# Five re-orderings in a four-layer network kernel: stacks at every step, v's products ahead of scores, sums for two groups, two copies on one engine, the mix ahead of transposes

## The chip, the cores and the metric

The kernel runs on one core of a Trainium2 chip, in single precision. The metric is the device time of one execution in microseconds. The core has five engines with queues of their own: TensorE (PE, matrix products and transposes, which write to eight PSUM banks), VectorE (DVE), ScalarE (ACT), GpSimd (POOL) and SyncE (SP), which here issues nearly all DMAs. Each engine takes its instructions in the order in which they were put into its queue.

## The reference

An input x of shape (2, 1024, 1024) passes through four layers. Each layer is an attention-like block and a feed-forward block, and each block ends in `x = layernorm(x + block(x))`. Cut to what the change touches:

```python
# layer 0, attention: 8 heads of 16, keys from all 1024 rows
qk = (x @ Wqk_w.T + Wqk_b).reshape(b, n, H, E, 2)          # q and k
v = (x @ Wv_w.T + Wv_b).reshape(b, n, H, E)
attn = softmax(einsum('bhqd,bhkd->bhqk', q, k)) / sqrt(128)
out = einsum('bhsl,bhlv->bhsv', attn, v) @ Wo_w.T + Wo_b
# layer 0, feed-forward: columns of x permuted, 16 blocks of up, gelu, down
# layer 1, attention: a convolution of width 3 over the rows (1024 -> 768), then attention in
# blocks of 128 rows with 16 heads of 64, output and projection
# layer 1, feed-forward: softmax router over 8 experts scales the input and output channels of
# x @ sign(weight).T
# layer 2: a selective state-space scan, then an int4 weight product
# layer 3, attention: one head of width 256 over 1024 rows
attn = softmax(einsum('bqd,bkd->bqk', q, k) / 16)
out = einsum('bqk,bkd->bqd', attn, v) @ Wo + bo
# layer 3, feed-forward: x @ base_W.T + b and low-rank experts weighted by the router's ranks
```

## The kernel before

The two batches run one after the other through all layers. A batch's x lies in SBUF as eight row tiles of 128 x 1024 (`x`), and a transposed copy as `xT` (eight column groups `k` of 128 by 1024 rows). `to_xT(tt)` makes the transposed copy of one row tile: eight PE transposes into two PSUM banks, and two copies out by `evac`, which gives them to DVE and ACT in turn. Inside a stage the order of the calls in the program is the order of the instructions on every engine; the stages are written out by hand. `ps()` takes one of the eight PSUM banks.

**Layer 0, attention (`l0`).** `qkv(s, th, scalar)` makes k, q or v (s = 1, 0, 2) for half th of the rows: eight k, two matmuls each, and gives way after every second k. The q and k parts are then spread over 32-row strips by eight small DMAs. `side` is the list of such pieces that are still to be made when the scores begin, one list entry for each step of a piece. `maxima(th)` makes the scores and their row maxima in 16 steps: in each, four matmuls of a step to come into four banks and four DVE reductions of the present one. The loop over n runs these steps and takes one piece of `side` after each (two in the first two steps). `attend(th, extra)` then makes scores again, exponentials and outputs in 16 steps, and runs the functions in `extra[n]` at step n: for th = 0 the steps of `maxima(1)`, for th = 1 (the second pass) the output projection, layernorm and `to_xT` of the first four row tiles. At the end of the second pass four stores `xd<-xT` put these tiles into DRAM, one at each of its steps 6 to 9, and at step 9 eight indirect DMAs on POOL (`gather(0)`) read them back with permuted columns (`t<-xd`). `blocks(th, ...)` is the feed-forward part; its first products need the first of these. Each of its blocks ends in a scatter to `yd` from POOL.

**Stacks.** In batch 0 alone, `stacks()` prepares layer 1's convolution weights: in 24 rounds it loads three pieces of 128 x 256 by SP, forms four sums with eight POOL operations, and stores them to the DRAM tensor `cvd` by SP. It is a generator of 26 steps: one loads, 24 store the round before, load the next and make the present one, and the last stores. It works in two sets of buffers. It is driven by `next(made)` at chosen steps of `maxima(0)`, of the first pass and of the second pass.

**Layer 1, attention (`l1_attn`).** The convolution is done in fast form. `sums(th, steps, k0, k1)` makes the input combinations on DVE, called `one`, `two`, `three` and so on; tile 1 of `one` is a + 2 and tile 2 becomes 2 - a. `product(co, j)` multiplies combination j with the weights of output group co over eight k (PE, line 740). At the start of the stage the tiles 4 to 7 of x still wait for their layer-0 output: it comes by scatters into `yd`, a reload into `vh`, and transposes in `add_y(tt, ys)`. Weights come through a ring of eight buffers. At the end `join(1)` makes the second half's outputs, and `to_xT(3)` and the first router product of `l1_ffn` (line 118, over tiles 0 to 3) follow.

**Layer 3 (`late_rest`).** For each of the eight row tiles: `scores`, `exps` (softmax with the maximum), `turn` (transposes of the weights into `pts`, copies by ACT). `mix(th)` multiplies `pts` of four tiles with v (32 matmuls in two banks, copies by `evac`), `join(wo, tt)` makes the output projection and adds it to x, `stats(tt)` makes mean and reciprocal root (DVE, then Ln and Exp on ACT, then four small DVE operations, line 186 first), `ln_scale(tt)` applies them on DVE, and `turn_x(tt)` is `to_xT(tt)` and the adding of a row vector on POOL (line 143). `route(0)` needs tiles 0 to 3 of `xT`.

Of the kernel before, what the change touches and what calls it, by code (L numbers as in the profile page):

```python
# [21 lines left out]
NT = S // P  # L22
# [5 lines left out]
class Net:  # L28
# [98 lines left out]
        if b < B:  # L127
            self.nc.sync.dma_start(self.x[:, tt, :], self.i["x"][b, tt * P : (tt + 1) * P, :])

    def to_xT(self, tt):  # L130
        nc = self.nc
        for g in range(2):
            p = self.ps()
            for j in range(4):
                k = 4 * g + j
                nc.tensor.transpose(p[:, j * P : (j + 1) * P], self.x[:, tt, k * P : (k + 1) * P], self.ident)  # L136
            self.evac(
                self.xT[:, 4 * g : 4 * g + 4, 1 + tt * P : 1 + (tt + 1) * P],
                p.rearrange("p (k t) -> p k t", k=4),
            )  # L140
# [79 lines left out]
    def l0(self, b):  # L220
        nc, i = self.nc, self.i
# [15 lines left out]
        with self.tc.tile_pool(name=self.nm("l0a"), bufs=1) as lp, self.tc.tile_pool(name=self.nm("l0b"), bufs=2) as tp:  # L237
# [346 lines left out]
            def at(extra, n, f):  # L584
                extra.setdefault(n, []).append(f)

            got = {}
            with self.tc.manual_schedule():
                self.table()
                for s in (1, 0):  # L590
                    for _ in qkv(s, 0, False):
                        pass
                for tt in range(4, NT):
                    self.to_xT(tt)
                for tt in range(4, NT):
                    self.add_row(row, tt)
                side = [
                    f for s, th in ((1, 1), (0, 1), (2, 0), (2, 1)) for f in [qkv(s, th, True)]
                    for _ in range(5 if s == 2 else 4)
                ]  # L600
                m0 = maxima(0)
                for n in range(16):
                    next(m0)
                    if b == 0 and n == 6:
                        made = stacks()
                    if b == 0 and n >= 6 and n % 3:
                        next(made)
                    for f in side[: 2 if n < 2 else 1]:
                        next(f)
                        del side[0]  # L610
                for f in side:
                    next(f)
                m = maxima(1)
                turns = {n: [lambda: next(m)] for n in range(16)}
                turns[0].insert(0, lambda: next(m0))
                if b == 0:
                    for n in range(16):
                        if n % 3:
                            turns[n].append(lambda: next(made))
                done0 = attend(0, turns)  # L620
                e = line(0, project, (0, 1, 3, 4, 5, 6, 7, 8, 9))
                e[0].insert(0, lambda: next(m))
                if b == 0:
                    for n in range(16):
                        if n % 3 < 2 and n < 14:
                            at(e, n, lambda: next(made))
                for n in range(4):
                    at(e, 6 + n, lambda n=n: store(n))
                at(e, 9, lambda: gather(0))
                ahead = {n: [lambda tt=tt: turn_o(tt)] for tt, n in enumerate((0, 1, 3, 4))}  # L630
                done = attend(1, e, ahead, lambda: done0(1))
                e = line(1, project, (0, 0, 1, 1, 2, 3, 3, 4, 4))
                for n, tt in ((3, 4), (3, 5), (4, 6), (4, 7)):
                    at(e, n, lambda tt=tt: store(tt))
                for n in (5, 6):
                    at(e, n, lambda: gather(1, 2))
# [14 lines left out]
    def l1_attn(self, b, yd, op):  # L651
        nc, i = self.nc, self.i
        row = self.row("l1_projb")
        with self.tc.tile_pool(name=self.nm("l1a"), bufs=1) as lp, self.tc.tile_pool(name=self.nm("l1s"), bufs=2) as spool:
# [47 lines left out]

            d = [("d", n) for n in range(6)]

            one = [(2, d[2], -4, d[4]), ("a", d[1], -4, d[3]), (1, "a", 1, 2), (2, "a", -1, 2)]
            two = [(4, d[2], -1, d[4]), ("b", d[1], -1, d[3]), (3, "b", 2, 4)]
            c_, e_ = ("c", d[2], -1, d[0]), ("e", d[3], -1, d[5])
            three, five = [(0, "c", 4, 4), (4, "b", -2, 4)], [(5, "b", -4, "e")]
# [86 lines left out]
            def product(co, j):  # L795
                c[co]["calls"](j)
# [5 lines left out]
            with self.tc.manual_schedule():  # L802
                if b == 0:
                    nc.vector.tensor_scalar(cb6, cb, -6.0, None, ALU.mult)
                    nc.vector.tensor_scalar(bq8, bq, 0.125, None, ALU.mult)
                for co, j in (
                    [(co, j) for j in (1, 2, 3, 0, 4) for co in (0, 1)] + [(2, 1), (2, 2), (2, 3), (0, 5), (1, 5)]
                    + [(2, 4), (2, 0), (2, 5)] + [(co, j) for co in (3, 4, 5) for j in ORDER]
                ):
                    c[co]["load"](j)  # L810
                pump()
                ys = [t for q in range(4) for t in (vh[:, q, :HALF], vh[:, q, HALF:])]
                for k, t in enumerate(ys):
                    nc.sync.dma_start(t, yd[k * P : (k + 1) * P, :])
                for k0, k1 in ((0, 2), (2, 4), (4, KD)):
                    sums(0, one, k0, k1)
                    c[0]["calls"](1, k0, k1)
                product(1, 1)
                product(0, 2)
                product(1, 2)  # L820
                sums(0, two)
                product(0, 3)
                product(1, 3)
                sums(0, [c_] + three)
                self.add_y(4, ys)
                root(4)
                product(0, 0)
                product(1, 0)
                self.add_y(5, ys)
                product(0, 4)  # L830
                c[0]["both"]()
                product(1, 4)
                c[1]["both"]()
                self.to_xT(4)
                sums(0, [e_] + five)
                root(5)
                for j in (1, 2, 3):
                    product(2, j)
                self.add_y(6, ys)
                for co in (0, 1):  # L840
                    product(co, 5)
                    c[co]["last"]()
                self.to_xT(5)
                root(6)
                product(2, 4)
                self.add_y(7, ys)
                product(2, 0)
                c[2]["both"]()
                product(2, 5)
                c[2]["last"]()  # L850
                self.to_xT(6)
                root(7)
                later = {
                    (3, 4): [lambda: self.to_xT(7)], (3, 5): [lambda: sums(1, [c_] + one)], (4, 2): [lambda: sums(1, two)],
                    (4, 4): [lambda: sums(1, [e_])], (5, 2): [lambda: sums(1, three + five)],
                }
                for co in (3, 4, 5):
                    for j in ORDER:
                        product(co, j)
                        if j == 0:  # L860
                            c[co]["both"]()
                        for f in later.get((co, j), []):
                            f()
                    c[co]["last"]()
# [171 lines left out]
            with self.tc.manual_schedule():  # L1036
# [49 lines left out]
                for tt in range(3):  # L1086
                    self.add_row(row, tt)
                join(1, wo)
                self.to_xT(3)
                self.add_row(row, 3)  # L1090
                early.append(row)
        return lambda tt, nh: project(tt, nh, wp), early
# [711 lines left out]
    def turn_x(self, tt, row):  # L1804

        self.to_xT(tt)
        self.add_row(row, tt)
# [243 lines left out]
    def late_rest(self, b, lp, tp, qk, v):  # L2051
        nc, i = self.nc, self.i
        NR = 15
        if True:
# [166 lines left out]
            with self.tc.manual_schedule():  # L2221
# [6 lines left out]
                for n in range(1, NT + 1):  # L2228
                    exps(n - 1)
                    if n >= 7:  # L2230
                        self.ln_scale(n - 7)
                    if n < NT:
                        scores(n)
                    if n == 5:
                        mix(0)
                    if n >= 6:
                        join(wo, n - 6)
                        stats(n - 6)
                    if n == NT:
                        join(wo, 3)  # L2240
                    turn(n - 1)
                    if n >= 7:
                        turn_x(n - 7, row)
                self.ln_scale(2)
                stats(3)
                turn_x(2, row)
                self.ln_scale(3)
                mix(1)
                turn_x(3, row)
                probs = route(0)  # L2250
                join(wo, 4)
# [161 lines left out]
```

## Time and profile before

| | us |
|---|---|
| median of 3 runs | 4809.61 (4804.67 to 4822.28) |
| the profiled execution's own time | 4813.16 |
| its span, from first to last instruction | 4811.4 |
| PE busy | 4440.4 (92%), mean granted clock 0.973 |
| DVE busy | 3331.1 (69%) |
| POOL busy | 2278.4 (47%) |
| ACT busy | 2031.3 (42%) |

The profile is that of one execution. Its timeline gives, for every group of like instructions, the start and the duration in us, the engine, the line of the kernel, the operation, output and inputs, the shape, the count, and in brackets how long the engine had been idle before and which engine's instruction or DMA ended that. "SPq" rows are DMAs that SyncE issues; their duration is that of the issuing. A table by windows gives the busy time of PE, weight loading (PEld), DVE, ACT and POOL in a stretch, the clock that TensorE was granted (1.00 is full), the share of the DMA engines' time, and GB/s.

### The profile page before, as it was taken

The numbers are of one execution on the slowest core, as the hardware profiler recorded it, in microseconds if no ns is written. First come the engines' busy times: TensorE is split into PE (matmuls) and PEld (weight loads), VectorE is DVE, ScalarE is ACT, GpSimd is POOL, SyncE is SP. The second block draws the span as 40 slices with busy tenths as digits, with TensorE's granted clock in tenths as the row PEclk, the third lists the DMA queues.
The fourth block names the chain that finished last, engine by engine and source line by source line (L and its number), as shares of the span: only waits on it lengthen the run. The fifth ranks groups of instructions, "written<-read, shape, count | busy, mean of one in ns | idle before, by whom it ended". The sixth has DMA issues, their size and how long they took to land.

```text
span 4811.4 us, 52825 instructions
## 1 busy us (share of the span) xinstructions
PE 4440.4 (92%) x17736; PEld 2192.6 (46%) x17736; DVE 3331.1 (69%) x4568; ACT 2031.3 (42%) x4131; POOL 2278.4 (47%) x1469
## 2 busy tenths in 40 slices
PE   9899999988898889999999999998888888899999
PEld 4367655333333333564443776553333333335644
DVE  5564276399999997645365643744999999966553
ACT  2432342577675653122025223325776756521310
POOL 5822121288798985030021121304888989841310
PEclk9999999999998999999999999999999999999999
DMA  4565314588888998310121742125888899993100
GB/s 154 158 225 174 108 63 136 146 220 226 237 217 236 252 253 262 127 56 37 53 71 56 244 160 81 64 96 148 223 226 235 210 246 253 246 287 97 54 13 31
DMA packets 315507, 768.08 MB, mean 160 GB/s; under 512 B 40288, under 2 KB 112096, under 8 KB 315236
## 3 DMA queue, kind: packets, MB, share of 16 engines
q1 hardware_dynamic: 307556, 739.52, 53.4%
q0 software_dynamic: 7680, 25.17, 1.6%
q8 instruction: 142, 2.33, 0.2%
q14 instruction: 129, 1.06, 0.1%
HBM read 644.75 MB, written 100.93 MB: 155 GB/s over the span
## 4 chain that ended last, share of the span: by engine, by line
PE 52%; DVE 17%; DMA 10%; issue 5%; POOL 5%; ACT 4%; SPq 1%; POOLq 0%; DVEq 0%; ACTq 0%
PE ps L110 15%; DVE h L1524 9%; PE ps L740 5%; PE ps L2206 5%; PE ps L1896 5%; POOL h L1510 3%; DMA h<-dxd 3%; PE ps L1632 2%; PE ps L1909 2%; PE ps L1850 2%; DVE h L1535 2%; DMA xi<-xcd 2%; PE ps L1546 2%; PE ps L136 1%; PE ps L1517 1%
## 5 line engine op out<-in xcount | busy, mean ns | idle before, releaser
L1510 POOL TENSOR_TENSOR h<-h,br 128x1024 f32<-128x1024 f32 x512 | 1206.2, 2373 | 108.4 <-DMA h<-dxd 68.8
L1519 ACT ACTIVATE ps<-ps,l_Alog 128x512 f32<-128x512 f32 x1024 | 663.1, 662 | 552.8 <-PE ps L1517 550.2
L1517 PE MATMUL ps<-hl,rep 128*128 128x512 f32 x1024 | 733.0, 720 | 171.7 <-DVE h L1524 142.1
L1524 DVE TENSOR_TENSOR_SCAN h<-ps,hst,h 128x512 f32<-128x512 f32 x512 | 628.5, 1263 | 23.0 <-ACT ps L1519 18.4
L1535 DVE TENSOR_TENSOR h<-h,ps 128x1024 f32<-128x1024 f32 x512 | 609.4, 1190 | 2.5 <-ACT hst L1532 2.4
L1524 DVE TENSOR_TENSOR_SCAN h<-ps,h 128x512 f32<-128x512 f32 x512 | 597.1, 1203 | 19.0 <-ACT ps L1519 19.0
L1632 PE MATMUL ps<-xT,w 128*128 128x512 f32 x1024 | 541.2, 614 | 9.4 <-DVE h L1524 8.2
L1517 PEld LDWEIGHTS ps<-hl,rep 128*128 128x128 f32 x1024 | 200.4, 197 | 593.7 <-DVE h L1524 424.8
L143 POOL TENSOR_TENSOR x<-x,row 128x1024 f32<-128x1024 f32 x80 | 190.8, 2406 | 572.5 <-PE ps L136 547.5
L949 POOL TENSOR_TENSOR s<-s,l1r 128x512 f32<-128x512 f32 x64 | 66.3, 1041 | 542.7 <-DVE l1r L948 500.4
L1670 PE MATMUL ps<-w,w 128*128 128x512 f32 x512 | 280.3, 632 | 23.3 <-DMA w<-yd 14.9
L1546 PE MATMUL ps<-h,sel 128*32 128x512 f32 x2048 | 294.8, 628 | 6.7 <-DVE h L1535 6.7
L1455 POOL TENSOR_TENSOR e<-e,one 128x512 f32<-128x512 f32 x64 | 81.6, 1275 | 434.7 <-ACT xp L1327 313.4
L1632 PEld LDWEIGHTS ps<-xT,w 128*128 128x128 f32 x1024 | 188.7, 193 | 200.8 <-issue 163.9
L1577 PE MATMUL ps<-xT,w 128*128 128x512 f32 x512 | 272.3, 631 | 6.2 <-DVE h L1524 6.2
L1335 DVE SCALAR_TENSOR_TENSOR ps<-xp,l_convw,ps 128x512 f32<-128x512 f32 x192 | 144.8, 754 | 183.8 <-ACT ps L1330 179.3
L158 DVE TENSOR_TENSOR x<-x,ps 128x512 f32<-128x512 f32 x192 | 128.6, 681 | 183.8 <-PE ps L2212 136.2
L1896 PE MATMUL ps<-w,w 128*128 128x512 f32 x512 | 228.3, 593 | 0.0
L183 ACT ACTIVATE rs<-mv 128x1 f32<-128x1 f32 (+2 forms) x78 | 15.9, 203 | 502.6 <-DVE mv L177 502.2
L2206 PE MATMUL ps<-w,xT 128*128 128x512 f32 x512 | 225.9, 593 | 0.0
L110 PE MATMUL ps<-xT,w 128*128 128x512 f32 x512 | 225.1, 592 | 0.0
L371 DVE TENSOR_REDUCE mx<-ps 128x1 f32<-128x512 f32 x256 | 158.8, 682 | 46.0 <-PE ps L361 46.0
(320 smaller groups left out, 7788.5 us busy)
## 6 DMA issues: line engine op xcount, KB each, us to landing
h<-dxd SPq DMA_DIRECT2D x512, 512.0 KB, 7.8
w<-l_in SPq DMA_DIRECT2D x128, 512.0 KB, 6.1
w<-cvd SPq DMA_DIRECT2D x96, 512.0 KB, 4.2
w<-l_out SPq DMA_DIRECT2D x96, 512.0 KB, 8.1
w<-l_conv SPq DMA_DIRECT2D x48, 512.0 KB, 4.2
w<-l_fw SPq DMA_DIRECT2D x32, 512.0 KB, 5.4
xcd<-xo SPq DMA_DIRECT2D x64, 256.0 KB, 6.5
xi<-xcd SPq DMA_DIRECT2D x64, 256.0 KB, 8.6
```

The lines of the kernel that those rows point to most:

```text
L110: self.nc.tensor.matmul(out, lhsT, rhs, start=j == 0, stop=j == n - 1)
L1510: nc.gpsimd.tensor_tensor(hs[k], hs[k], norms[of(k)[0]][1].unsqueeze(1).to_broadcast([P, 2, HALF]), ALU.mult)
L1517: nc.tensor.matmul(dA[k, m], rep[:, 4 * m + q, :], hl[u, c][:, jj, :], start=True, stop=True)
L1519: nc.scalar.activation(dA[k, m], dA[k, m], AF.Exp, scale=A[:, g : g + 1])
L1524: nc.vector.tensor_tensor_scan(hs[k][:, m, :], dA.pop((k, m)), hs[k][:, m, :], hst[:, g : g + 1] if u else 0.0, ALU.mult, ALU.add)
L1535: nc.vector.tensor_tensor(hs[k], hs[k], norms[of(k)[0]][3].unsqueeze(1).to_broadcast([P, 2, HALF]), ALU.mult)
L1546: nc.tensor.matmul(py[u, c][32 * j : 32 * j + 32, :], self.sel[:, q, :], hs[k - 1 + j // 2][:, j % 2, :], start=False, stop=q == 3,)
L1577: nc.tensor.matmul(p, w["w"][:, k * P : (k + 1) * P], self.xcols(k, u0, HALF), start=k == 0, stop=k == KD - 1)
L1632: nc.tensor.matmul(p, w["w"][:, k * P : (k + 1) * P], self.xcols(k, u * HALF, HALF), start=k == 0, stop=k == KD - 1)
L1670: nc.tensor.matmul(p, y[:, cc, t * P : (t + 1) * P], wt[:, cc * HALF : (cc + 1) * HALF], start=c2 == 0 and cc == 0, stop=last,)
L1896: nc.tensor.matmul(pa[tt], y[:, cc * HALF + tt * P : cc * HALF + (tt + 1) * P], w[:, cc * HALF : (cc + 1) * HALF], start=c2 == 0 and cc == ...
L2206: nc.tensor.matmul(p, self.xcols(k, tt * P, P), wt[k][:, ns], start=k == 0, stop=False)
```

## The change

Five places are re-ordered; nothing that is computed changes.

1. `stacks()` is advanced at every step from step 6 of `maxima(0)` on and at every step of the first pass, and no more in the second pass. Before it was advanced at two steps of three in all three places. (Batch 0.)
2. The first three steps of v's first half (six of its eight k) are run ahead of `maxima(0)`; the list `side` keeps its length, so that its last entries for this piece do nothing. (Batch 0.)
3. In layer 1, each of the three portions of sums is followed by the products of two output groups, not one, and the fourth sum of `one` (now `less`) is made after the three portions, over all k at once.
4. `to_xT(3)` at the end of layer 1's attention uses DVE for both copies.
5. In layer 3, `mix(1)` is put ahead of the layernorm and transposes of tiles 2 and 3, and at the last step `stats(2)` behind `turn(7)`.

```diff
-    def to_xT(self, tt):
+    def to_xT(self, tt, evac=None):
...
-            self.evac(
+            (evac or self.evac)(
...
+                if b == 0:
+                    for _ in range(3):
+                        next(side[8])
                 m0 = maxima(0)
                 for n in range(16):
                     next(m0)
                     if b == 0 and n == 6:
                         made = stacks()
-                    if b == 0 and n >= 6 and n % 3:
+                    if b == 0 and n >= 6:
                         next(made)
                     for f in side[: 2 if n < 2 else 1]:
-                        next(f)
+                        next(f, None)
                         del side[0]
...
                 if b == 0:
                     for n in range(16):
-                        if n % 3:
-                            turns[n].append(lambda: next(made))
+                        turns[n].append(lambda: next(made))
                 done0 = attend(0, turns)
                 e = line(0, project, (0, 1, 3, 4, 5, 6, 7, 8, 9))
                 e[0].insert(0, lambda: next(m))
-                if b == 0:
-                    for n in range(16):
-                        if n % 3 < 2 and n < 14:
-                            at(e, n, lambda: next(made))
                 for n in range(4):
                     at(e, 6 + n, lambda n=n: store(n))
                 at(e, 9, lambda: gather(0))
...
-            one = [(2, d[2], -4, d[4]), ("a", d[1], -4, d[3]), (1, "a", 1, 2), (2, "a", -1, 2)]
+            one = [(2, d[2], -4, d[4]), ("a", d[1], -4, d[3]), (1, "a", 1, 2)]
+            less = [(2, "a", -1, 2)]
...
                 for k0, k1 in ((0, 2), (2, 4), (4, KD)):
                     sums(0, one, k0, k1)
                     c[0]["calls"](1, k0, k1)
-                product(1, 1)
+                    c[1]["calls"](1, k0, k1)
+                sums(0, less)
                 product(0, 2)
...
-                    (3, 5): [lambda: sums(1, [c_] + one)],
+                    (3, 5): [lambda: sums(1, [c_] + one + less)],
...
-                self.to_xT(3)
+                self.to_xT(3, nc.vector.tensor_copy)
...
                     if n >= 6:
                         join(wo, n - 6)
-                        stats(n - 6)
+                        if n < NT:
+                            stats(n - 6)
                     if n == NT:
                         join(wo, 3)
                     turn(n - 1)
+                    if n == NT:
+                        stats(2)
                     if n >= 7:
                         turn_x(n - 7, row)
+                mix(1)
                 self.ln_scale(2)
                 stats(3)
                 turn_x(2, row)
                 self.ln_scale(3)
-                mix(1)
                 turn_x(3, row)
                 probs = route(0)
```

More of the change, by code (lines that the diff above doesn't have):

```diff
@@ L605, in l0 @@
                         made = stacks()
-                    if b == 0 and n >= 6 and n % 3:
+                    if b == 0 and n >= 6:
                         next(made)
                     for f in side[: 2 if n < 2 else 1]:
-                        next(f)
+                        next(f, None)
                         del side[0]
                 for f in side:
-                    next(f)
+                    next(f, None)
                 m = maxima(1)
@@ L853, in l1_attn @@
                 later = {
-                    (3, 4): [lambda: self.to_xT(7)], (3, 5): [lambda: sums(1, [c_] + one)], (4, 2): [lambda: sums(1, two)],
+                    (3, 4): [lambda: self.to_xT(7)], (3, 5): [lambda: sums(1, [c_] + one + less)], (4, 2): [lambda: sums(1, two)],
                     (4, 4): [lambda: sums(1, [e_])], (5, 2): [lambda: sums(1, three + five)],
```

## The prediction

> **What bounds the kernel now.** I read the page first: one core, TensorE (PE) busy 92% of the span, so a change that only reorders its work can win no more than the idle pieces in front of the moved steps, and half-speed stretches of its clock. The span against which everything below is summed:
>
> ```profile
> span 4811.4 us, 52825 instructions
> ```
>
> Then the timeline of PE, for the five places. A row is start, duration, engine, line, operation, count, and in brackets the idle time before it and what ended that.
>
> ```profile
> 32.74 5.63 PE L361 MATMUL ps<-kT,qT 32*128 32x512 f32 x16 [4.67 <-DMA qT<-st]
> 220.90 3.79 PE L514 MATMUL ps<-t,w 64*128 64x512 f32 x8 [9.66 <-DMA t<-xd,idx]
> 313.02 13.05 PE L740 MATMUL ps<-qh,w 128*128 128x128 f32 x88 [1.92 <-DVE qh L699]
> 653.39 2.05 PE L118 MATMUL ps<-xT,l_gate 128*32 128x512 f32 x16 [0.35 <-DVE xT L103]
> 2232.55 1.97 PE L136 MATMUL ps<-ident,x 128*128 128x128 f32 x8 [5.96 <-DVE x L192]
> ```
>
> These are the first scores (4.67 us), the first blocks (9.66), the sums (1.92, after pieces of 2.23 and 1.08), the router (0.35) and the layernorm chain of the last attention (5.96). The first two are in batch 0 alone; the others recur about 2389 us later. Third, the timelines of GpSimd (POOL) and of the DMA queue (SPq) before the largest wait, and one stretch of the table by windows:
>
> ```profile
> 140.00:160.00 20.00, 18.39 (x155) 7.11 (x153) 12.81 (x26) 8.52 (x17) 18.54 (x25) 1.00 0.45 143
> ```
>
> ```profile
> 210.42 2.14 SPq L280 DMA_DIRECT2D w<-l_conv  x3
> 212.68 0.38 SPq L486 DMA_DIRECT2D xd<-xT  x1
> 214.38 0.72 POOL L291 TENSOR_TENSOR w<-w 128x256 f32<-128x256 f32 x1
> 216.92 1.18 POOL L496 DMA_INDIRECT t<-xd,idx  x1 [1.82 <-DMA xd<-xT]
> 226.86 0.83 POOL L284 TENSOR_TENSOR w<-w 128x256 f32<-128x256 f32 x1
> 239.25 0.73 POOL L291 TENSOR_TENSOR w<-w 128x256 f32<-128x256 f32 x1
> ```
>
> In 20 us POOL (the fifth pair) is busy 18.54; the rest is 0.08 us between operations. The stacks run back to back on it from 71.13: 22 of 24 stand ahead of the gather at 216.92, the last two (226.86 to 239.98) behind it.
>
> **Stacks at every step.** No operation is added. Before, calls stood at 6 + 10 + 10 steps; now at 10 + 16, all 26 before the second attention pass begins. So POOL has 24 stacks ahead of the gather, not 22, and the queue of SP has all their stores ahead of the four stores xd<-xT, which the gather reads. Emitting earlier does not run them earlier, since POOL has no gap: 22 stacks took 71.13 to 215.10, 6.54 each, so two more end at 215.10 + 13.1 = 228.2. Before, from the issue of the last xd store to PE's first product is 220.90 - 212.68 = 8.22. Now the last stack store goes out at the stack's end, and the four xd stores behind it at about 0.45 each.
>
> **v's products ahead.** Twelve matmuls (six k, two each) move into the 4.67 wait. In this stage 32 took 14.01, 0.438 each: 5.25, so PE is 0.6 late for the scores. What it buys is the clock, which the windows from 34 to 42 us give as 0.50. Batch 1 has the same steps without the idle piece:
>
> ```profile
> 44.14 1.14 PE L361 MATMUL ps<-kT,qT 32*128 32x512 f32 x8
> 48.84 1.14 PE L361 MATMUL ps<-kT,qT 32*128 32x512 f32 x8
> 2438.46 3.53 PE L361 MATMUL ps<-kT,qT 32*128 32x512 f32 x16
> 2450.26 1.14 PE L361 MATMUL ps<-kT,qT 32*128 32x512 f32 x8
> ```
>
> From the first scores to this point it takes 16.10 at half clock (32.74 to 48.84) and 11.80 in batch 1. The gain is 4.3 less 0.6, say 3.8. The twelve matmuls taken out at steps 6 to 8 give about 1 us more, as VectorE's (DVE) four reductions (2.48 a step) then set the pace. v's sum holds one of 8 PSUM banks for six more steps; the next scores take two free banks and two that the first two reductions (1.24) free within a step of 2.98, so I cost that at nothing, and at up to 6 x 1.24 if that cover fails. None of this reaches the end by itself: PE only comes earlier to the gather. It counts through the stacks: the q stores that stand ahead of their first load on SP go out 3.8 earlier, so 228.2 becomes 224.4. The xd stores then issue from 224.8 to 226.2. One alone lands in about 4.0; in the pairs of the trace the second lands 1.2 later than a lone one. Landing of the last: 230.2 if they don't slow each other, 234.3 if each further one adds 1.8 (1.2 and the 0.6 between a pair's issues). From there 0.28 to the gather and 3.98 to PE: 234.5 to 238.5. I take 237.4, near the slow end, as all four start within 1.4 us. Against 220.90: **+16.5** (13.6 at the least; 17.6 + 3.8 = 21.4 if v moves the stacks by nothing). PE's wait grows from 9.7 to some 30 us. What follows (blocks, scatters, l1) is in PE's order and shifts with it; the two stacks that stood ahead of the first yd scatter (240.13) delayed no PE, so their going pays nothing.
>
> **Sums for two groups.** The same products, interleaved; the fourth sum is made once for all eight k behind the third chunk. DVE's total stays, and "two" is ready when it was, about 318.6. Before, PE came to its products after 318.6 because its clock was 0.50 until about 319; now the double portions fill two of the three gaps and PE ends the group about 3.4 earlier (318.6 + 32 x 0.112 = 322.2 against 325.6 in batch 1's spacing). But the next step needs vh:
>
> ```profile
> 309.19 6.93 DMA yd<-w,idx
> 319.95 8.58 DMA vh<-yd
> 328.57 0.33 PE ps L150
> ```
>
> That is the chain of waits of batch 0: PE waits for the scatter and reload, untouched by this edit. Gain 0 there, and the longer idle (6.3 with little between) drops the clock for the next 3 to 7 us: +1.7 to +3.4, taken as 2.2. In batch 1 vh lands by about 2714.4, PE is done at 2712.2: -1.7 (0 to -3.4), +0.5 for the clock. Together **+1.0** (-3.4 to +5).
>
> **Both copies of to_xT(3) on DVE.** DVE idled 6.14 us before the first copy; the second ends at 653.9 where ScalarE's (ACT) ended at 654.3. The router's second four k come 1 us into its products, so PE did not wait for it: **0** (-0.3 to +0.7 if DVE weren't free), both batches.
>
> **Mix ahead of transposes.** mix(1) fills the 5.96: it starts at about 2226.4 instead of 2234.3, at full clock; 32 such matmuls took 14.00 (L110 at 638.17), so to 2240.4. stats(2) behind turn(7) also lets ACT make the mix's inputs by 2226.4. What is queued behind: ln_scale(2) and stats(3) stand on DVE behind the mix's first copy (2233.4), harmless; but stats(3)'s Ln stands on ACT behind the second copy (2240.4 + 0.6), so rsqrt starts on DVE at about 2241.5, just when POOL adds the row to tile 2:
>
> ```profile
> 2234.60 2.35 POOL L143 TENSOR_TENSOR x<-x,row 128x1024 f32<-128x1024 f32 x1 [5.59 <-PE ps L136]
> 2234.63 2.34 DVE L186 TENSOR_TENSOR rsq<-rs 128x1 f32<-128x1 f32 x1 [0.50 <-ACT rs L184]
> 2237.00 0.16 DVE L187 TENSOR_TENSOR rsq<-rsq,mv 128x1 f32<-128x1 f32 x1
> ```
>
> One element per partition takes 2.34 instead of 0.16: it ends with POOL's add. So again: POOL to 2243.7, three operations 0.6, tile 2's copy 0.67, ln_scale(3) 0.8, PE at 2245.8. Before, tile 3's transposes began at 2249.66: -3.9; in batch 1 by the same offsets -3.3 (4636.13 before). This wait of 4.6 us is new and takes the place of the 5.96. The old one was followed by a clock of 0.50 from about 2231 to 2237; a new half-speed stretch costs 1.7 to 3.4 each: I take 2.1. Together **-3.0** for both batches (-8 without cold clock, 0 if it eats all).
> The Trainium skill (SBUF — State Buffer, section "Who interferes with whom") says that a VectorE instruction with two SBUF inputs and a GpSimd instruction that reads SBUF exclude each other, the first holding the ports to its end; that speaks against this order, and the row agrees with it. Without the rule the edit would be worth about 1.8 more per batch.
> The skill's TensorE: Matmul & The Clock Gate (Part 1) has the clock fall after a whole idle window of about 3.4 us. By it 4.6 idle need not hold such a window and the part would be nearer -7; here the table shows 0.50 at 310 to 318 after idle pieces of 2.23 and 1.08 with products between, so I keep the fall.
>
> **Sum.** 16.5 + 1.0 + 0 - 3.0 = 14.5 on the profiled execution: its span goes from 4811.4 to 4825.9. That execution's own time, 4813.16, lies 3.55 above the median 4809.61; on the median that is 4824.
>
> **Rivals.** (1) Slower by over 0.5%: the four xd stores and the stack's last stores land one after another. Place: SP's queue at 224 us. Price: four times 4.0 behind 224.8 is 240.8, PE at 245, +24, with the other parts +22 to +27: 4832 to 4837. It decides once the landing takes over some 17 us. For it: all leave at once; against: pairs overlap in the trace. (2) Faster: the stacks are out of the way when the second pass ends, as the edit's name has it. Then 9.66 and half of the 6 cold us after it go: -13, with the mix -16 (-24 with all ends low): 4786 to 4797. It decides if the 24 stacks end before PE is done with the pass (about 206): 138.7 us from 67.3, or 5.8 a stack against 6.54. The 18.54 busy of 20 speaks against it. (3) Stacks as forecast, mix and sums at their best (-8, -3): +5, 4815.
>
> **How the numbers follow.** Forecast with (3), from +4 to +24: 0.74; (1) 0.16; (2) 0.10, of which 0.04 beyond 24 us. The ends of the terms give 13.6 - 3.4 - 0.3 - 8 = +2 to 21.4 + 5 + 0.7 = +27; runs of one kernel spread -5 to +13. Range 4806 to 4837; it leaves out most of (2) and the top of (1). About 0.5% (24 us) is what a measurement of this kernel can tell from no change: faster 0.04, within 0.80, slower 0.16.
>
> **What would show it.** The gather's first row behind all 24 stacks, at about 234, xd stores at about 225, PE's wait before L514 near 30: right. A gather before 217: the stacks step is wrong. No 0.50 at 34 to 42 and the first stack at 67: v right. A wait of about 4.6 before tile 3's transposes behind the mix, with a stretched L186: mix right. vh still ends the wait of batch 0's sums. A time below 4800 makes the whole wrong.

## The result and the profile after

The changed kernel takes 4826.88 us (median of 19 runs, 4809.98 to 4839.54). The kernel before takes 4815.21 beside it (19 runs, 4804.67 to 4822.28). The ratio is 1.0024, 95% interval 1.0017 to 1.0032: some 12 us slower, within the 0.5% that the forecast named. The forecast was 14.5 us more. The profiled execution has a time of 4823.02 and this span, 9.9 longer than before's:

```profile
span 4821.3 us, 52833 instructions
```

The timeline of TensorE (PE) after, at the places shown for before (start, duration, engine, line, operation, shape, count, idle before and what ended it). Lines behind the sums are one lower in the changed kernel: L740 is L739.

```profile
28.62 5.32 PE L317 MATMUL ps<-xT,w 128*128 128x512 f32 x12
33.87 3.03 PE L361 MATMUL ps<-kT,qT 32*128 32x512 f32 x16
45.16 1.14 PE L361 MATMUL ps<-kT,qT 32*128 32x512 f32 x8
238.43 3.79 PE L514 MATMUL ps<-t,w 64*128 64x512 f32 x8 [29.71 <-DMA t<-xd,idx]
341.15 0.33 PE L150 MATMUL ps<-ident,vh 128*128 128x128 f32 x1 [1.07 <-DMA vh<-yd]
668.02 1.93 PE L118 MATMUL ps<-xT,l_gate 128*32 128x512 f32 x16 [0.35 <-DVE xT L137]
2243.44 13.90 PE L110 MATMUL ps<-pt,v 128*128 128x512 f32 x32
2262.69 1.56 PE L136 MATMUL ps<-ident,x 128*128 128x128 f32 x8 [4.48 <-DVE x L192]
```

The 4.67 us before the first scores are gone and the scores run at full clock. The wait before the first blocks has grown from 9.66 to 29.71. The 5.96 before tile 2's transposes is filled by the mix, and a new wait of 4.48 stands before tile 3's. Behind the largest wait stand these rows of GpSimd (POOL) and of SyncE's DMA queue:

```profile
223.83 0.72 POOL L291 TENSOR_TENSOR w<-w 128x256 f32<-128x256 f32 x1
225.00 4.05 SPq L486 DMA_DIRECT2D xd<-xT  x4
234.72 1.18 POOL L496 DMA_INDIRECT t<-xd,idx  x1 [10.17 <-DMA xd<-xT]
```

The 24th stack ends at 224.55 and the first starts at 67.83, so a stack takes (224.55 - 67.83) / 24 = 6.53 us, as before. Only then do the four xd stores leave, and GpSimd waits 10.17 more for them to land.

To see where the rest went, every PE operation of the two traces was paired in order, and the difference of its start taken. The position of the changed kernel against before's:

| place | difference, us | step |
|---|---|---|
| second pass ends (208) | -2.5 | |
| first blocks (220.90 before) | +17.5 | +20.1 |
| end of the blocks | +16.9 | -0.7 |
| first products that need vh | +14.6 | -2.2 |
| router behind `to_xT(3)` | +14.5 | -0.1 |
| ahead of the mix, batch 0 | +17.0 | +2.5 |
| behind the router of the mix, batch 0 | +14.3 | -2.7 |
| ahead of the sums, batch 1 | +14.1 | -0.2 |
| behind the sums, batch 1 | +11.7 | -2.4 |
| ahead of the mix, batch 1 | +12.4 | +0.8 |
| behind the mix, batch 1 | +10.3 | -2.2 |

Layer 2, which no edit touches, lies in the rows "ahead of the mix". Between 1290 and 1340 us alone, the thirteen other kernels moved against before's profile by -2.5 to +5.3, so single spans can't settle effects of a few us. Positions right behind an edit say more, but each profile is one execution too.

### The profile page after: what moved, and what is told of

The parts are those of the page before. It is cut to its first block, busy times and chain, and to the rows that moved or that the text cites. A ratio compares the mean times of both kernels' runs of the same rounds, so it can differ in the third digit from the quotient of the medians.

```text
span 4821.3 us, 52833 instructions
## 1 busy us (share of the span) xinstructions
PE 4422.1 (92%) x17736; PEld 2180.7 (45%) x17736; DVE 3338.7 (69%) x4566; ACT 2028.6 (42%) x4129; POOL 2276.8 (47%) x1469
## 4 chain that ended last, share of the span: by engine, by line
PE 56%; DVE 17%; DMA 9%; issue 5%; POOL 4%; ACT 3%; SPq 1%; DVEq 0%; POOLq 0%; ACTq 0%
PE ps L110 16%; DVE h L1524 10%; PE ps L739 5%; PE ps L2206 5%; PE ps L1896 5%; DMA h<-dxd 3%; PE ps L1632 3%; POOL h L1510 3%; PE ps L1909 2%; DVE h L1535 2%; PE ps L1850 2%; PE ps L1546 2%; PE ps L136 2%; PE ps L1670 2%; PE ps L1517 2%
## 5 line engine op out<-in xcount | busy, mean ns | idle before, releaser
L1517 PE MATMUL ps<-hl,rep 128*128 128x512 f32 x1024 | 719.9, 707 | 191.8 <-DVE h L1524 157.9
L1524 DVE TENSOR_TENSOR_SCAN h<-ps,h 128x512 f32<-128x512 f32 x512 | 598.5, 1208 | 18.4 <-ACT ps L1519 18.3
```

Of the source, the lines that this page charges most:

```text
L1517: nc.tensor.matmul(dA[k, m], rep[:, 4 * m + q, :], hl[u, c][:, jj, :], start=True, stop=True)
L1524: nc.vector.tensor_tensor_scan(hs[k][:, m, :], dA.pop((k, m)), hs[k][:, m, :], hst[:, g : g + 1] if u else 0.0, ALU.mult, ALU.add)
```

## The experiments

**Theory and rivals.** The theory was that of the forecast: GpSimd works its stacks without a gap, so calling them earlier only puts two more stacks and their DMAs ahead of the gather; the other four edits win a little. Rivals: another part of the change causes the loss; the density of the calls, not their number, does; or one of the two queues (GpSimd's or SyncE's) is all of it. Results in one table, with the first blocks' start in the profile:

| kernel | ratio to before (95%) | first blocks, us |
|---|---|---|
| before | 1 | 220.90 |
| the change | 1.0024 (1.0017 to 1.0032) | 238.43 |
| stacks_only | 1.0045 (1.0030 to 1.0059) | 240.44 |
| v_only | 0.9987 (0.9977 to 0.9997) | 215.53 |
| dose22 | 1.0005 (0.9996 to 1.0014) | 222.89 |
| pool24 | 1.0025 (1.0015 to 1.0034) | 229.91 |
| xd_act | 1.0048 (1.0034 to 1.0063) | 243.50 |
| mix_only | 0.9994 (0.9986 to 1.0003) | 219.54 |
| sums_only | 0.9996 (0.9986 to 1.0007) | 218.95 |
| no_stacks | 0.9980 (0.9972 to 0.9989) | 216.25 |
| best20 | 0.9975 (0.9966 to 0.9984) | 207.05 |
| best20ln | 0.9948 (0.9936 to 0.9961) | 211.01 |
| best21ln | 0.9951 (0.9937 to 0.9964) | 208.73 |
| early23ln | 0.9942 (0.9928 to 0.9955) | 212.56 |

Before's own profile is late at this place: its first stack starts at 71.13, that of the five other kernels without the second edit at 69.1 to 69.9. mix_only and sums_only, which leave layer 0 as it was, reach their first blocks 1.4 and 2.0 us earlier than before. Differences of first blocks under some 2 us therefore show nothing.

**stacks_only: the first edit alone.**

```diff
-                    if b == 0 and n >= 6 and n % 3:
+                    if b == 0 and n >= 6:
...
-                        if n % 3:
-                            turns[n].append(lambda: next(made))
+                        turns[n].append(lambda: next(made))
...
-                if b == 0:
-                    for n in range(16):
-                        if n % 3 < 2 and n < 14:
-                            at(e, n, lambda: next(made))
```

> The kernel before with the first edit alone: stacks at every step. Theory (GpSimd is the bound: 24 stacks of 6.54 us stand ahead of the gather instead of 22, and the four xd stores stand behind their stores): the last stack ends at 71.13 + 24 x 6.54 = 228.1, and in the changed kernel PE restarted 13.9 us after the last stack's end, so at 242.0 against 220.90: +21 at the first blocks, +18 to +21 in the time. Rival 1 (most of the changed kernel's loss came from elsewhere, from v or from the sums): +5 or less. Rival 2 (the stacks are out of the way at the end of the second pass): -10 or more.

Measured: +0.45%, some 22 us. Its PE timeline:

```profile
240.44 3.79 PE L514 MATMUL ps<-t,w 64*128 64x512 f32 x8 [30.50 <-DMA t<-xd,idx]
```

That is +19.5 at the first blocks; this run's stacks began at 69.79 rather than 71.13, which is most of what the forecast of +21 was off. The stacks edit alone costs more than the whole change: rivals 1 and 2 fall.

**dose22: as dense, but 22 ahead.** Calls at every step, 13 in the first pass, and the last three behind the gather.

```diff
+                    for n in range(13):
+                        turns[n].append(lambda: next(made))
...
+                    for n in (10, 12, 13):
+                        at(e, n, lambda: next(made))
```

> The kernel before with stacks called at every step, but again only 22 of 24 ahead of the gather; the last three calls follow the gather as before. All stores of those 22 stand ahead of the four xd stores on SyncE's queue. Theory 1 (the number of stacks ahead of the gather sets the loss, and the bunched xd stores add a part): the 22nd stack ends at 215.1 as before; the xd stores are issued together from about 212.7 instead of one by one, and with the 9.4 us that they took to land in the changed kernel the gather comes at 222.4 and PE at 226.1: +5. Theory 2 (bunching costs nothing, only the count): within 1 of before. Rival (calling the stacks more densely is what costs, whatever the count): +15 or more.

Measured: 1.0005, no difference. The profile has the small part that theory 1 gave to the bunched stores:

```profile
209.51 4.00 SPq L486 DMA_DIRECT2D xd<-xT  x4
222.89 3.60 PE L514 MATMUL ps<-t,w 64*128 64x512 f32 x8 [13.07 <-DMA t<-xd,idx]
```

The four stores leave together and the gather starts 9.1 us later, at 218.63. PE is 2.0 later than before with stacks that began 1.7 earlier, so bunching costs 2.0 to 3.7 against the 5 expected. The density of the calls costs nothing else: the number ahead of the gather decides.

**pool24: 24 stacks on GpSimd, the stores ahead of the last two on SyncE.**

```diff
-                        if n % 3 < 2 and n < 14:
+                        if n % 3 < 2 and n < 10:
...
                     at(e, 6 + n, lambda n=n: store(n))
+                if b == 0:
+                    for _ in range(3):
+                        at(e, 9, lambda: next(made))
```

> The kernel before with one edit: the last three calls of the stacks stand between the last xd store and the gather, not behind the gather. So 24 stacks are ahead of the gather on GpSimd, as in the changed kernel, but the xd stores keep their place ahead of the last two stacks' DMAs on SyncE. It parts the +19.5 us that the stacks edit alone cost at the first blocks. Theory (two causes of like size: two stacks on GpSimd, and the xd stores behind the stacks' DMAs): the 24th stack ends at 71.13 + 24 x 6.5 = 227, the gather follows at once, PE starts the blocks at 231 to 232: +10 to +11, time +9 to +12. Rival 1 (the stores behind SyncE's queue are nearly all of it): +5 or less. Rival 2 (GpSimd's two stacks are nearly all): +17 or more.

Measured: 1.0025, some +12. GpSimd's gather and PE's first blocks:

```profile
226.31 1.18 POOL L496 DMA_INDIRECT t<-xd,idx  x1 [0.17 <-issue]
229.91 3.41 PE L514 MATMUL ps<-t,w 64*128 64x512 f32 x8 [20.16 <-DMA t<-xd,idx]
```

The gather follows the last stack at once. With both kernels' stacks beginning near 69.5 (69.11 here, 69.79 in stacks_only), +9.0 of the +19.5 is the wait on GpSimd and +10.5 is the stores' place on SyncE with their landing. Counted from each kernel's own first stack, so without before's late start, the two parts are 11.0 and 9.9. Two causes of like size; both rivals fall.

**xd_act: the changed kernel with the four xd stores issued by ScalarE.**

```diff
-                nc.sync.dma_start(
+                (nc.sync if tt // 4 else nc.scalar).dma_start(
                     xd[tt // 4]...
```

> The changed kernel with one more change: the four xd stores of the first half are issued by ScalarE instead of SyncE, so that they do not stand behind the stacks' stores. The gather still stands behind 24 stacks on GpSimd. Theory (the loss has two parts, GpSimd's two stacks and SyncE's queue with the landing of four stores at once): stores leave near 198, the gather starts when the 24th stack ends, at about 224.9, and PE at 228.6 instead of 238.4: -10 against the changed kernel, about +2 against before. Rival 1 (the stacks on GpSimd set all of it): PE within 2 of 238, time +10 to +12 against before. Rival 2 (the stores slow ScalarE's exponentials): the second pass ends later than 208.7.

Measured: 1.0048, so some 12 us worse than the change where 10 us better was expected: a miss. ScalarE's timeline and SyncE's queue say why:

```profile
212.87 0.38 SPq L295 DMA_DIRECT2D cvd<-third  x1
215.29 0.38 ACTq L486 DMA_DIRECT2D xd<-xT  x1
215.72 2.06 ACT L404 ACTIVATE pt<-ps 128x512 f32<-128x512 f32 x4 [31.70 <-DMA cvd<-third]
```

ScalarE stood still for 31.70 us, with the exponentials of the second pass behind it, until a stack's store had landed. In this profile the DMAs of SyncE and ScalarE share eight semaphores, taken in turn in the order of the program. The first xd store has that of the store of 212.87, eight DMAs ahead, and ScalarE waits for this semaphore until 215.19. So giving the store to another engine did not take it out of the line. The second pass ended 32 us later than before, and the first blocks follow it at 243.50 without a wait: that is the sign that rival 2 named, by another way than its own. The parting of the two queues rests on pool24 alone.

**v_only.** The second edit on the kernel before.

```diff
+                if b == 0:
+                    for _ in range(3):
+                        next(side[8])
```

> The kernel before with v's six k ahead of the scores, nothing else. Theory (v counts only through the stacks): PE ends the second pass 2 to 3 us earlier, the first stack starts near 67.3 instead of 71.13, all 22 stacks and the gather come 3.8 earlier: PE's first blocks at 217.1 against 220.90, time -3 to -4. Rival 1 (the gather is not set by the stacks' start): PE's wait before the first blocks grows by as much as PE gains, time within 1 of before. Rival 2 (the PSUM bank held by v costs steps): +1 to +7.

Measured: 0.9987, some -6 (-1 to -11). First stack at 66.50, first blocks -5.4: theory right in kind, larger in size than its 3.8, because the stacks began 4.6 earlier than in before's profile. Of this, 1.2 to 2.0 is before's own late start.

**mix_only.** The fifth edit on the kernel before (diff as in the change).

> The kernel before with the mix ahead of transposes alone (both batches). Theory, from the changed kernel's trace, where this part took -2.7 us in the first batch and -2 to -2.5 in the second by the position of the work behind it: -5, between -2 and -7; a wait of 4.5 us ahead of tile 3's transposes in each batch with a rsq of 2.3 us (line 186). The record's number for this part is -3.0. Rival (the wait eats all of it): 0.

Measured: 0.9994, some -3 (-7 to +1). Right behind the edit its PE moved by -2.7 in batch 0 and -2.0 in batch 1; the same places moved by -2.7 and -2.2 in the changed kernel.

**sums_only.** The third edit on the kernel before.

> The kernel before with the sums for two groups alone. The record has +1.0 for this part: 0 in the first batch by the path through vh, +2.2 there for a colder clock, -1.2 in the second batch. Theory after the changed kernel's trace: the first batch 0 (vh ends the wait with and without the edit, and no half-speed piece follows it), the second -2.4 to -3.3, as in the three kernels with the edit: -2.5 in all. Rival (the clock's fall in the first batch is real): +2 or more behind the sums of the first batch. The time itself can't tell -2.5 from +1 well; the positions in the profile must.

Measured: 0.9996 (-7 to +3 us), which by itself tells nothing, so the positions must. From the first products of the sums to the first that need vh, the five kernels without the edit (stacks_only, dose22, v_only, mix_only, pool24) take 18.1 to 18.7 us in both batches. Before's profile has 20.6 in batch 0, where its reload of vh took 8.58 us against 6.5 to 7.0 in the others, and 18.4 in batch 1. With the edit there are two lengths. It is 15.0 to 16.0 where vh is there in time: in batch 1 of the change and of five more, and in batch 0 of best21ln and of sums_only, whose transposes of vh follow with no wait:

```profile
320.94 1.04 PE L150 MATMUL ps<-ident,vh 128*128 128x128 f32 x8
```

It is 18.0 to 18.7 where vh comes last: in batch 0 of the change and five more, and in batch 1 of sums_only, where the expectation had its gain (and 20.2 in batch 1 of xd_act). So the theory's two values are right and the batch is not what decides: the edit wins some 2.4 to 3.4 us when vh is early and nothing when it isn't. By this measure the rival falls: no kernel is 2 us longer in batch 0 than those without the edit. But the measure ends at the first products that need vh. Just there the clock does fall in three other kernels with the edit, so the rival holds in some executions (see the part on the prediction). Why vh is early in one place and late in another stays open.

**no_stacks: the change without its first edit.**

> The changed kernel with the first edit undone: stacks paced as before, the other four edits kept. Theory (the parts add up): v -6.2 (its own run), sums -2.5, mix -4.6 (by the positions in the profiles) or -2.9 (its own run), both copies on one engine 0: -12 to -13, time near 4801 if before is near 4814; first blocks near 215.5 to 217, as with v alone. Rival (what v wins at the gather is lost again at vh or later): -5 to -8.

Measured: 0.9980, some -10 (-5 to -13), between theory and rival and nearest to the sum of the parts' own runs (v -6.3, sums -1.9, mix -2.9: -11). With stacks_only at +22 the parts add up to +11; the change measured +12.

**best20: fewer stacks ahead.** Edits 2, 3 and 5 on the kernel before, and the stacks moved the other way.

```diff
+                    for n in range(11):
+                        turns[n].append(lambda: next(made))
...
+                if b == 0:
+                    for n in (0, 1, 2, 3, 4):
+                        at(e, n, lambda: next(made))
                 blocks(0, e, ahead, lambda: done(1))
```

> Edits 2, 3 and 5 of the change (v, sums, mix) on the kernel before, and the stacks paced the other way: 10 calls in the first scores, 11 in the first pass, none in the second pass, and the last five behind the first five scatters of the blocks. So 20 stacks, not 22 or 24, are ahead of the gather. Theory: the 20th stack ends at 66.8 + 20 x 6.5 = 197, the last tile for the xd stores is ready near 198, the gather comes near 203, and its landing near 207 is about where PE ends the pass (208.7): PE starts the blocks at 209 against 220.90, -12; with -3 to -5 for sums and -5 for mix: -20 to -22, time 4795 to 4798. Rival (the four late stacks delay the scatters on GpSimd, and through yd and vh the sums): the gain at the first blocks is there but half of it or more is gone at the sums: -8 to -12.

Measured: 0.9975, some -12. The large wait is gone, but a part of it comes back at the second half's first block:

```profile
207.05 1.99 PE L514 MATMUL ps<-t,w 64*128 64x512 f32 x8
256.46 5.97 PE L514 MATMUL ps<-t,w 64*128 64x512 f32 x16 [4.59 <-DMA t<-xd,idx]
```

PE is 13.9 early at the first blocks and 8.3 early at their end. On GpSimd, the scatter of block 4 went out at 247.27, at once behind the last stack; the next one, at 251.80, and the second half's gathers after it. The rival was right about the way (late stacks delay scatters) and about the time, the theory about the place of the first gain.

**best20ln: layernorms ahead of the mix.**

```diff
-                mix(1)
                 self.ln_scale(2)
                 stats(3)
-                turn_x(2, row)
                 self.ln_scale(3)
+                mix(1)
+                turn_x(2, row)
                 turn_x(3, row)
```

> The same as the kernel with 20 stacks ahead, and in the last layer the layernorms of tiles 2 and 3 (with their Ln on ScalarE) put ahead of the mix, so that they do not stand behind the copies of the mix. Theory: the wait of 4.5 us ahead of tile 3's transposes goes (the layernorm is done some 3 us before the mix ends), and the half-speed piece after it: -5 to -6 for each of two batches, -11 in all against the kernel without it. Rival (the wait moves to another place, such as the copies of xT or the row sum on GpSimd): -3 or less.

Measured: 0.9948, 10 to 13 us faster than best20 (by the medians and by the ratios). Its PE timeline:

```profile
2222.93 13.90 PE L110 MATMUL ps<-pt,v 128*128 128x512 f32 x32
2236.67 1.91 PE L136 MATMUL ps<-ident,x 128*128 128x128 f32 x16
```

Sixteen transposes follow the mix with no wait. By position the mix part is now -8.6 and -8.0 against -2.7 and -1.5 in best20. So the 4.48 us wait of the changed kernel came from this order. The edit takes two things away at once and does not part them: the Ln behind the mix's copy on ScalarE, and the rsq stretched to 2.32 us beside GpSimd's addition, which takes 0.16 here.

**best21ln and early23ln: where GpSimd is idle.** The first puts a 21st stack between the last xd store and the gather (GpSimd idled 5.89 us there in best20) and three behind scatters 0 to 2. The second also begins the stacks at step 2 instead of 6, so that 23 are ahead of the gather.

```diff
+                if b == 0:
+                    at(e, 9, lambda: next(made))
...
-                    if b == 0 and n == 6:
+                    if b == 0 and n == 2:
                         made = stacks()
-                    if b == 0 and n >= 6:
+                    if b == 0 and (n in (2, 3) or n >= 6):
```

> The kernel with 20 stacks ahead and the layernorms ahead of the mix, with one more edit: a 21st stack is called between the last xd store and the gather, where GpSimd stood idle for 6 us, and the other three behind the scatters of blocks 0 to 2, not 0 to 3. With the stack behind scatter 3, the scatter of block 4 went out at 247.3, and as each scatter waits for the one before it to land (some 4.5 us), the second half's gathers came late and PE waited 4.6 us. Theory: the first blocks stay at 207 to 211, and the wait of 4.6 us falls to 1 or less: -3 to -4 against the kernel with 20 ahead. Rival 1 (the gather comes later by the 21st stack): the first blocks begin 2 us or more later, and nothing is won. Rival 2 (the wait has another cause): it stays at 4.6.

> The kernel with 21 stacks ahead of the gather and the layernorms ahead of the mix, with one more edit: the stacks begin at step 2 of the first scores, not at step 6 (calls at steps 2 and 3, then from 6 on), so that GpSimd works where it stood idle from 39 to 66 us, and the first loads stand ahead of the q stores of step 5 on SyncE. Two more stacks fit ahead of the gather (23), and one stands behind the first scatter of the blocks. Theory (GpSimd's stretch of 24 stacks has only to begin earlier): first stack near 54 instead of 66.3, gather at 204 as before, no stack behind scatters 1 and 2, PE's wait before the second half's first block falls from 3.8 us to 1 or less: -3 to -5 against the kernel with 21 ahead, -27 to -31 against before. Rival 1 (the q stores come late behind the stacks' stores): PE waits in the first pass or the second scores, and it is slower than the kernel with 21 ahead. Rival 2 (that wait is set by the scatters' own landings, about 5 us each, not by the stacks): the wait stays above 3 us and the time within 2 us of the kernel with 21 ahead.

Measured: 0.9951 and 0.9942, not to be told from 0.9948 or from each other. In best21ln the later wait stays; in early23ln it goes, and the first stack starts at 54.39 as expected:

```profile
257.93 5.19 PE L514 MATMUL ps<-t,w 64*128 64x512 f32 x16 [3.76 <-DMA t<-xd,idx]
```

```profile
255.63 3.70 PE L514 MATMUL ps<-t,w 64*128 64x512 f32 x16 [0.49 <-DMA t<-xd,idx]
```

In best21ln the scatters behind the last stack (241.83, 247.41, 253.19) are still 5.6 to 5.8 apart, and 3.76 us of best20ln's wait of 4.58 stayed, as rival 2 had it. With one stack, behind scatter 0, the data for the second half came 2.3 earlier although the blocks began 3.8 later, and PE itself came 1.0 later. So the stacks behind scatters 1 and 2 are most of the cause. early23ln's second pass, though, ended 4.5 later than best21ln's and its gather came at 208.0, not at 204, so it lost there what it won behind. These three kernels are some 24 to 28 us faster than before, where the change is 12 slower.

## Why the prediction was right, and where it was not

**Stacks at every step with v: +16.5, measured +17.5 at the first product and +16.9 behind the blocks.** Right by its own steps: the 24th stack at 224.55 for 224.4, the gather behind all of them at 234.72 for 234, the wait 29.71 for 30. The working had the four stores leave within 1.4 us; they took 4.05 to issue, and the last landed at 233.83, near the slow end of the bounds. stacks_only, dose22 and pool24 show the mechanism: two more stacks on GpSimd and the stores behind them on SyncE, about half each. The closeness of the size is in part luck: the forecast was worked out from before's profile with its late stacks, and against the first blocks of mix_only and sums_only (219.54, 218.95) the change is some 19 later.

**v ahead: 3.8 earlier, measured 3.7** at the scores. The first stack came 3.3 earlier, not 3.8. Over all profiles whose stacks begin at step 6, it starts at 65.8 to 67.8 in the seven with the edit and at 69.1 to 71.1 in the six without: some 3 earlier. PE's end of the second pass came only 2.5 earlier, for a reason that the working did not have: a new fall of the clock (below). It cost the change little, since PE waited there anyway.

**Sums for two groups: +1.0, measured -2.4 by position.** This is the term that was mis-sized. Batch 0 was right in that vh ends the wait; the +2.2 for a colder clock did not come here. The windows of the changed kernel (PE, PEld, DVE, ACT and POOL busy, clock, DMA share, GB/s) have it at full speed:

```profile
325.00:345.00 20.00, 15.17 (x119) 13.60 (x120) 16.68 (x17) 0.00 (x0) 1.08 (x1) 1.00 0.83 297
```

PE's idle pieces stayed short (1.52 and 0.77 between the products, at most 1.07 while it waited for vh), and batch 1 gained 2.4 rather than 1.2. The colder clock was no mistake in kind, though. With the edit vh ends the wait of batch 0 in six kernels. In three of them (xd_act, best20ln, early23ln) the clock falls to 0.50 at the end of this wait, for 3.4 to 6.8 us, and PE loses 1.6 to 2.6 us by it. In the other three (the change, no_stacks, best20) it does not. What decides it stays open. The -2.2 in the table at vh is no gain of the edit: the kernels without it have it too, because the reload was slow in before's profile.

**Both copies on DVE: 0, measured -0.1.**

**Mix ahead: -3.0, measured -4.9 by position** (its own run: -3, interval -7 to +1). The steps came out one by one: ScalarE's Ln behind the second copy, the rsq on VectorE stretched by GpSimd's addition.

```profile
2257.86 0.21 ACT L183 ACTIVATE rs<-mv 128x1 f32<-128x1 f32 x1
2258.29 2.34 POOL L143 TENSOR_TENSOR x<-x,row 128x1024 f32<-128x1024 f32 x1 [12.27 <-PE ps L136]
2258.33 2.32 DVE L186 TENSOR_TENSOR rsq<-rs 128x1 f32<-128x1 f32 x1 [4.78 <-ACT rs L184]
```

Tile 3's transposes came 4.0 and 3.4 earlier against the work before them, for 3.9 and 3.3. The clock fell behind the wait, as the working kept it, but it cost 1.25 in each batch (from -4.0 to -2.7, from -3.4 to -2.2) instead of 2.1: that size is what was off.

**The sum.** +14.5 was forecast, +9.9 is the difference of the spans, +12 that of the medians. Sums and mix together were 5.3 better than put, and the two spans differ by a few us in layer 2. **Rivals:** (1) fell, since the stores overlap (the last of the four landed 8.8 us after the first was issued); (2) fell, since a stack took 6.53 and not 5.8 us; (3), mix and sums at their best, went half of its way: -7.3 together, where it had -11 (its -8 for the mix is more than the 3.9 + 3.3 = 7.2 of the working).

## What to carry to other kernels

Where an engine works its queue without a gap, calling its work earlier in the program does not make it earlier; it only moves what stands behind it, so count what is ahead of the transfer that is next on the path, on each queue. To win, look for that engine's idle stretches and put the work there (here GpSimd before the first stack, or between the last store and the gather), and put small steps that the next tile needs ahead of a long product, not behind its copies. A DMA that is given to another engine may still wait for its turn behind earlier ones, and stop that engine meanwhile.

## What the runs showed of the hardware that was not expected

**TensorE's clock fell without an idle window.** With v's products gone from steps 6 to 8, the scores of 32 rows stand alone for some 9 us. The windows of the changed kernel:

```profile
54.67:61.50 6.83, 6.83 (x35) 2.31 (x28) 5.32 (x10) 1.37 (x2) 0.00 (x0) 1.00 0.10 21
61.50:68.33 6.83, 6.83 (x30) 3.34 (x29) 6.69 (x14) 0.65 (x2) 0.50 (x1) 1.00 0.51 135
68.33:75.15 6.82, 6.82 (x15) 2.56 (x16) 4.56 (x10) 0.00 (x0) 6.25 (x10) 0.50 0.19 61
```

The profile models the ends of matmuls and counts PE as busy in all three stretches; behind the second, which is nearly only 32-row scores, the clock is at 0.50 for 6.83 us. PE does not work at its peak in the second, though. In best20, at full clock, the 32 scores take 8.41 us, where the eight of a step before take 1.14. VectorE, busy for 6.69 of the 6.83, sets their pace. Of the eight kernels with v ahead, seven show such a fall near 67 to 70 us. PE's position afterwards (at 90 us) goes with its length: -2.5 to -3.4 where it lasts 6.8 us (five kernels), -4.2 and -5.0 where it lasts 3.4, -6.1 in best20, where there is none. The Trainium skill (TensorE: Matmul & The Clock Gate, Part 1) ties the lower clock to an idle window of some 3.4 us; in the second stretch no two matmuls start more than 0.6 us apart, so no such window stands ahead of this fall. Whether the slower pace or the few rows in use bring it about is not shown: no run parts them.

**Scatters from GpSimd to one tensor go one landing at a time.** In best21ln three of them follow at 241.83, 247.41 and 253.19, with GpSimd idle 4.55 and 4.82 us between. In best20, whose profile has landings, the scatter of 247.27 landed at 251.07 and the next went out at 251.80. So one stack of 6.5 us that delays one of them delays those that follow.
